# Precedence for PSUM evictions, longer holds in the planner and two zero products at the start

## The chip, the cores and the metric

The kernel runs on one core of one Trainium2 chip. The core has TensorE (PE, matrix products into PSUM), VectorE (DVE), ScalarE (ACT), GpSimd (POOL) and SyncE (SP, which issues DMAs); each takes its own instructions in the order in which the build laid them down. The metric is the device time of one execution in microseconds, the median of the runs shown; lower is better.

## What is computed

Four sequences of 1024 tokens with 256 features pass two layers, in float32. Each of the four sublayers is `x = layernorm(x + f(x))`.

```python
x = ln(x + ssd(x))         # state-space mixing: 2 heads of 128, state 64, causal in a sequence
x = ln(x + gelu(x @ w1 + b1) @ w2 + b2)          # hidden width 1024
x = ln(x + linear_attention(x))  # 16 heads of 16, features exp(clip(norm(q or k) @ omega)), 64 per head
x = ln(x + shared_ffn(x) + routed_ffn(x))  # 2 shared experts, and the best 2 of 8; hidden 512, silu gate
```

The attention is causal: with features `qf`, `kf` each token's output is `sum(qf.kf * v) / sum(qf.kf)` over the tokens up to it, carried from chunk to chunk of 128 tokens as a running state.

## The kernel before

**Tiling.** The 4096 tokens are 8 blocks of 512 (4 tiles of 128). All of a block's activations stay in SBUF (`xs[i]`). The state-space part (`ssd_block`) and the feed-forward (`ffn_block`) work on blocks, the attention on 16 half blocks `hb` (`attn_front`, `attn_back`), `attn_tail` turns the result and computes the router's logits. Then `dispatch` and `invert` sort tokens by expert, the routed part (`slot_tiles`) works through 69 tiles of 128 sorted tokens, and the shared experts' products are cut into small jobs (`shared_jobs`) that are put wherever PE would otherwise be idle: blocks 0 to 2 ("early") and 3 to 5 ("amid") before the routed tiles, 6 and 7 ("late") after them. The jobs form one chain. A block's output products come after the load for the next block, and the amid blocks wait for the last attention projection (`proj_end[15]`), as they use the attention's PSUM banks.

**PSUM.** Until the routed part, PSUM is two pools of banks of 128 x 512 floats: 6 banks in pool 0 (state-space, attention, amid jobs) and 2 in pool 1 (feed-forward, early jobs). A product writes a bank, then ScalarE or VectorE copies or combines it into SBUF (an eviction), and the bank can be written again.

**The order on PE** is laid down by a planner, `trace_tasks`. Each piece of PE work is a `Task` with a cost, a rank, what it comes after (with a waiting time each), a pool and a number of banks, and a hold: the time for which its banks are counted as taken after its end, 1.5 if nothing is said. The planner keeps a clock, takes the task that can start first (the lower rank at equal starts) and so writes PE's instructions in that order:

```python
start = max([d.end + wait for d, wait in task.after], default=0.0)
for k in range(task.banks):
    start = max(start, free[task.pool][k] - task.cost * k / task.banks)
```

**The order on VectorE, ScalarE and GpSimd** is chosen by the tile framework's scheduler until the routed part ends: among instructions that could run, by its own estimate, the one that was written earlier goes first. `tc.high_priority(400)` lets an instruction count as written 400 places earlier.

**Names used below** (lines of the kernel before). In the feed-forward: `ps_txT` (transposes, L206) is copied to `xT` (L208); `ps_h` (L441) goes through Gelu to `hT` (L444); `ps_f` (L453) is added to `x` (L461). In the attention: `ps_txTa` (L206) to `xTa` (L208); `ps_qk` (L502) to `qk` (L505), squared, normalised through `rsqrt` and turned: `ps_qkT` (L550), copied to `qkT` (L551); `ps_p` (L564) to the features `qf`, `kf`, half by VectorE (L574) and ScalarE's exponential (L575), half by ScalarE's Relu (L577), exponential (L578) and VectorE (L579); `ps_sc` (L611) masked to `sc` (L620 to L623); `ps_k` (L633) to `kt` (L634); `ps_o` (L650) to `oraw` (L658); `ps_s` (L672) into `state` (L680, L682); `ps_kv` (L688) to `kv` (L689); `ps_to` (L695) divided into `o` (L698 to L701); `ps_oT` (L708) to `oT` (L710); `ps_w` (L715) added to `x` (L717). In the tail: `ps_txTr` (L206) to `xTr` (L208), `ps_l` (L758). Shared jobs: `ps_g` (L941), silu `sl` (L949), `gT` (L950), `ps_e` (L959), added to `x` (L968). The first products of all are `ps_bc` (L288), from `wx_sb` and the transposed input `xt`. ScalarE loads a table (`ACT_TABLE_LOAD`) when it passes between Gelu, Silu and the exponential; copies and Relu need none. `rsqrt` is a guess by integer arithmetic and three Newton steps, 11 VectorE instructions.

**The end.** The last block's jobs are written in a fixed order on PE, VectorE and ScalarE: after the addition L968 of its third tile come the layernorm sums and scales of the first three tiles, then the addition of the fourth.

Of the kernel before, what the change touches and what calls it, by code (L numbers as in the profile page):

```python
# [27 lines left out]
ALU = mybir.AluOpType  # L28
# [48 lines left out]
def two_layers(ctx: ExitStack, tc: tile.TileContext, x, xT, vecs, cols, wx, w1, w2, wqkv, wout, om, rw, moe, out):  # L77
# [42 lines left out]
    rw_sb = const.tile([P, KC, VW], F32, name="rw_sb")  # L120
    nc.sync.dma_start(out=wx_sb, in_=wx)
    nc.sync.dma_start(out=xts[0], in_=xT[0])
    nc.sync.dma_start(out=vec0, in_=vecs[:NVEC0].partition_broadcast(P))
# [59 lines left out]
    def rsqrt(v, shape, tag):  # L183

        r = sm.tile(shape, F32, tag=f"{tag}_r", name=f"{tag}_r")
        s = sm.tile(shape, F32, tag=f"{tag}_s", name=f"{tag}_s")
        nc.vector.tensor_single_scalar(s.bitcast(I32), v.bitcast(I32), 1, ALU.logical_shift_right)  # L187
        nc.vector.tensor_scalar(r.bitcast(I32), s.bitcast(I32), -1.0, float(0x5F3759DF), ALU.mult, ALU.add)  # L188
        for _ in range(3):
            nc.vector.scalar_tensor_tensor(s, r, -0.5, r, ALU.mult, ALU.mult)  # L190
            nc.vector.tensor_mul(s, s, v)  # L191
            nc.vector.scalar_tensor_tensor(r, s, 1.5, r, ALU.add, ALU.mult)  # L192
        return r

    def transposed(t, i, tiles, n, engines):


        width = len(tiles) * P
        engines = list(engines)
        for c0 in range(0, KC, 512 // width):  # L200
            chunks = range(c0, min(KC, c0 + 512 // width))
            ps = bank(f"ps_t{t.name}_{c0}", n)
            at = 0
            for c in chunks:
                for j in tiles:
                    nc.tensor.transpose(ps[:, at : at + P], xs[i][:, j, c * P : (c + 1) * P], ident)  # L206
                    at += P
            engines.pop(0)(t[:, c0 : chunks[-1] + 1, :].rearrange("p c t -> p (c t)"), ps[:, :at])  # L208
        return t
# [219 lines left out]
    def ffn_block(i, before, wk):  # L429
# [16 lines left out]
        def outputs(j):  # L446
            if j == 0:
                b2 = vec0[:, _VEC["b2"]].unsqueeze(1).to_broadcast([P, NT, D])
                nc.gpsimd.tensor_add(xs[i], xs[i], b2)
            if j % 2 == 0:  # L450
                v.ps = bank(f"ps_f{i}_{j}", 1).rearrange("p (s d) -> p s d", s=2)
            for m in range(HID0 // P):
                nc.tensor.matmul(  # L453
                    v.ps[:, j % 2, :],
                    v.hT[:, m, j * P : (j + 1) * P],
                    w2_sb[:, m, :],
                    start=(m == 0),
                    stop=(m == HID0 // P - 1),
                )
            if j % 2 == 1:  # L460
                nc.vector.tensor_add(xs[i][:, j - 1 : j + 1, :], v.ps, xs[i][:, j - 1 : j + 1, :])  # L461
            if j == NT - 1:
                layernorm(i)

        r = 10.0 + i
        last = Task(turn_x, 0.9, r, [(ssd_end[i], 10.0), (before, 0.0)], 1, 2)
        wait = 4.0
# [19 lines left out]
    def attn_front(hb, wk):  # L487
# [11 lines left out]
        def project(j):  # L499
            ps = bank(f"ps_qk{hb}_{j}", 0)  # L500
            for k in range(KC):
                nc.tensor.matmul(  # L502
                    ps, v.xT[:, k, j * P : (j + 1) * P], wqkv_sb[:, k, : 2 * D], start=(k == 0), stop=(k == KC - 1)
                )
            nc.vector.tensor_add(v.qk[:, j, :], ps, bq[:, : 2 * D])  # L505
            sq = wk.att.tile([P, 2 * D], F32, tag="sq", name=f"sq{hb}_{j}", bufs=2)
# [34 lines left out]
        def turn_qk(s):  # L541

            if s == 1:
                v.qkT = wk.att.tile([P, 4, TH], F32, tag="qkT", name=f"qkT{hb}", bufs=1)
            ps = bank(f"ps_qkT{hb}_{s}", 0)
            for q in range(2):
                for j in range(NJ):
                    at = (q * NJ + j) * P
                    c = 2 * s + q
                    nc.tensor.transpose(ps[:, at : at + P], v.qk[:, j, c * P : (c + 1) * P], ident)  # L550
            nc.scalar.copy(v.qkT[:, 2 * s : 2 * s + 2, :].rearrange("p c t -> p (c t)"), ps)  # L551

        def features(s):
# [17 lines left out]
            for r in range(4):  # L571
                f = ft[:, r].rearrange("p q t -> p (q t)")
                if r % 2 == 0:
                    nc.vector.tensor_scalar(f, ps[r], fcap, ffloor, ALU.min, ALU.max)  # L574
                    nc.scalar.activation(f, f, AF.Exp, bias=fbias[:, s : s + 1])  # L575
                else:
                    nc.scalar.activation(f, ps[r], AF.Relu, bias=fcap, scale=-1.0)  # L577
                    nc.scalar.activation(f, f, AF.Exp, bias=ecap[:, s : s + 1], scale=-1.0)  # L578
                    nc.vector.tensor_scalar_max(f, f, elow[:, s : s + 1])  # L579

        r = 5.0 + 0.1 * hb
        used = used_end.get(hb - 2)
        t_x = Task(turn_x, 0.45, r, [(qk_end.get(hb - 2), 0.0), (ffn_end[i], 10.0), (constants, 0.0), (attention, 0.0)], 0, 1)
        t_q = Task(lambda: project(0), 1.8, r, [(t_x, 3.5)], 0, 1)
        t_q = Task(lambda: project(1), 1.8, r, [(t_q, 0.0)], 0, 1)
        t_v = Task(values, 1.8, r + 0.1, [(t_x, 3.0), (used, 0.0)], 0, 1)
        t_k = Task(lambda: turn_qk(1), 0.45, r + 0.2, [(t_q, 12.0), (feat_end.get(hb - 1), 0.0)], 0, 1)
        t_q = qk_end[hb] = Task(lambda: turn_qk(0), 0.45, r + 0.2, [(t_k, 0.0)], 0, 1)
        t_k = Task(lambda: features(1), 0.95, r + 0.3, [(t_k, 5.0), (used, 0.0)], 0, 4, 4.5)
        feat_end[hb] = Task(lambda: features(0), 0.95, r + 0.3, [(t_q, 5.0), (t_k, 0.0), (t_v, 0.0)], 0, 4, 4.5)  # L590

    def attn_back(hb, wk):
# [5 lines left out]
        def scores(j):  # L598
# [7 lines left out]
            for q in range(2):  # L606
# [9 lines left out]
                for s in range(2):  # L616
                    t_s = t[:, 4 * s : 4 * s + 4, :]
                    ps_s = ps[s].rearrange("p (r t) -> p r t", t=P)
                    if (q, s) == (0, 0):
                        nc.scalar.copy(t_s, ps_s)  # L620
                        nc.gpsimd.tensor_mul(t_s, t_s, mask)  # L621
                    else:
                        nc.vector.tensor_mul(t_s, ps_s, mask)  # L623
                sc[j].append(t)

        def turn_keys(j):
# [3 lines left out]
            for q in range(2):  # L630
                ps = bank(f"ps_k{hb}_{j}_{q}", 0)
                for r in range(4):
                    nc.tensor.transpose(ps[:, r * P : (r + 1) * P], kf[:, r, q, tok], ident)  # L633
                nc.scalar.copy(kt[j][:, q, :], ps)  # L634

        def outputs(j):
# [20 lines left out]
            for n in range(2):  # L657
                nc.scalar.copy(  # L658
                    o[j].rearrange("p (g n t) -> p n g t", n=2, t=P)[:, n],
                    ps_o[n][:, : 2 * P].rearrange("p (g t) -> p g t", t=P),  # L660
                )

        def advance(j):
# [17 lines left out]
            else:  # L681
                nc.vector.tensor_add(state, ps_v[:, : 4 * NF], state)  # L682

        def turn_state(j):

            ps_kv = bank(f"ps_kv{hb}_{j}", 0)
            for q in range(2):
                nc.tensor.transpose(ps_kv[:, q * P : (q + 1) * P], state[:, q * 2 * NF : (q + 1) * 2 * NF], ident)  # L688
            nc.scalar.copy(kv.rearrange("p f e -> p (f e)"), ps_kv[:, : 2 * P])  # L689

# [14 lines left out]
        def turn_back(j):  # L705
# [3 lines left out]
            oT[j] = wk.att.tile([P, KC, P], F32, tag="oT", name=f"oT{hb}_{j}", bufs=2)  # L709
            nc.scalar.copy(oT[j].rearrange("p c t -> p (c t)"), ps[:, :D])  # L710

        def project(j):
# [3 lines left out]
            x_j = xs[i][:, j0 + j, :]  # L716
            nc.vector.tensor_add(x_j, ps[:, :D], x_j)  # L717
            if hb % 2 == 1 and j == NJ - 1:
                layernorm(i)

        for j in range(NJ):
# [5 lines left out]
            t_c = Task(lambda j=j: scores(j), 1.8, r, [(feat_end[hb], 7.0), (before.get("o"), 0.0)], 0, 4, 2.5)  # L727
            t_k = Task(lambda j=j: turn_keys(j), 0.9, r + 0.01, [(feat_end[hb], 6.0), (before.get("s"), 0.0)], 0, 2, 2.0)
            t_o = Task(
# [6 lines left out]
            t_t = at_tile[n]["to"] = Task(lambda j=j: turn(j), 0.45, r + 0.04, [(t_o, 1.5), (far.get("oT"), 0.0)], 0, 1, 2.5)  # L736
            t_t = at_tile[n]["oT"] = Task(lambda j=j: turn_back(j), 0.25, r, [(t_t, 2.0), (far.get("w"), 0.0)], 0, 1)
            t_w = at_tile[n]["w"] = Task(lambda j=j: project(j), 0.9, r, [(t_t, 2.5)], 0, 1)
        used_end[hb], proj_end[hb] = t_o, t_w

    def attn_tail(i, wk):
# [26 lines left out]
        r = 5.3 + 0.2 * i  # L768
        t_x = turn_end[i] = Task(turn_x, 0.9, r, [(proj_end[2 * i + 1], 10.0), (tail_end.get(i - 1), 0.0)], 0, 2)
        t_x = Task(logits, 0.5, r, [(t_x, 5.0)], 0, 1)  # L770
# [299 lines left out]

    def last_norm(i, tiles):

# [4 lines left out]
        r = None  # L1077

        def sums():
            st = sm.tile([P, NT, 6], F32, tag="ln_st", name=f"ln_st{i}_{tiles[0]}")  # L1080
            for k, j in enumerate(tiles):
                nc.vector.bn_stats(st[:, k, :], xs[i][:, j, :])  # L1082
                nc.vector.bn_aggr(mv[:, k, :], st[:, k, :])  # L1083

# [6 lines left out]
        def finish():  # L1091
# [7 lines left out]
            )  # L1099

        return sums, scales, finish

# [41 lines left out]
    early, amid, late = [0, 1, 2], [3, 4, 5], [6, 7]  # L1144
    with tc.manual_schedule(engines={mybir.EngineType.PE}):
        for i in range(NBLK):
            ssd_block(i, wk0)
# [97 lines left out]
    with tc.manual_schedule(  # L1245
# [8 lines left out]
        for _, kind, *_, piece in jobs:  # L1254
# [9 lines left out]
            if n in norm:  # L1264
                parts.extend(last_norm(*norm[n]))
                if len(parts) == 3:
                    parts.pop(0)()
            if n == 22:
                ends = last_norm(NBLK - 1, whole[:-1])
                ends[0]()  # L1270
                ends[1]()
# [74 lines left out]
```

## Time and profile before

| | us |
|---|---|
| median of 3 runs | 1566.04 |
| lowest, highest | 1563.34, 1570.9 |
| the profiled execution, its own time | 1570.37 |
| its span, first to last instruction | 1568.6 |
| PE busy in the span | 1493.9 |
| VectorE, ScalarE, GpSimd busy | 761.8, 599.2, 420.3 |
| mean granted TensorE clock (1 is full) | 0.983 |

The profile is of one execution. "Waits" name who waited for whom, with the total in us, the number of times and the longest one. In a timeline, the bracket behind an instruction is the idle time of its engine just before it and what ended that. One float32 matrix product shows as two passes (`x2`), a transpose as one. The granted clock of a stage is the mean over it.

### The profile page before, as it was taken

How to read it: one execution, taken by the hardware profiler on the slowest of the kernel's cores; microseconds unless marked ns; L12 is line 12 of the kernel's file. 1: busy time of each engine (PE TensorE's matmuls, PEld its weight loads, DVE VectorE, ACT ScalarE, POOL GpSimd, SP SyncE). 2: the span in 40 equal slices, each digit the busy share in tenths (PEclk: the TensorE clock that was granted, in tenths of full speed). 3: DMA queues.
4: the chain of work that ended last, by engine and by line, in shares of the span. 5: the costliest groups of instructions: out<-in, count | busy, mean ns of one | idle time of the engine just before them, and what ended most of it. 6: DMA issues, size and time to landing. Idle time of an engine off the chain costs nothing. (4 is left out here: it accounts for less than half of the span.)

```text
span 1568.6 us, 25398 instructions
## 1 busy us (share of the span) xinstructions
PE 1493.9 (95%) x9700; PEld 970.0 (62%) x9700; DVE 761.8 (49%) x2411; ACT 599.2 (38%) x1056; POOL 420.3 (27%) x456
## 2 busy tenths in 40 slices
PE   8999989999999989989999999999999999999997
PEld 5566647575857665755765765556666666666554
DVE  5977735665656475575455456122222222222264
ACT  3463373436364625446547411111222222222132
POOL 5623302322122121221110004012444444443100
PEclk9999999999999999999999999999999999999999
DMA  9000000000000000030101043041223223232431
GB/s 328 1 1 1 1 1 2 27 2 1 28 1 15 15 1 28 2 122 1 48 8 55 15 166 136 24 151 41 46 47 46 46 45 47 45 47 35 91 104 54
DMA packets 49654, 73.55 MB, mean 47 GB/s; under 512 B 8416, under 2 KB 42208, under 8 KB 48000
## 3 DMA queue, kind: packets, MB, share of 16 engines
q1 hardware_dynamic: 35856, 52.19, 9.4%
q0 software_dynamic: 13248, 18.17, 7.5%
q8 instruction: 80, 1.31, 0.4%
q10 hardware_dynamic: 432, 1.57, 0.3%
q14 instruction: 38, 0.31, 0.1%
HBM read 45.93 MB, written 25.99 MB: 46 GB/s over the span
## 5 line engine op out<-in xcount | busy, mean ns | idle before, releaser
L1013 PE MATMUL ps_ge<-w,xeT 128*128 x552 | 248.5, 593 | 1.0 <-issue 1.0
L941 PE MATMUL ps_g<-xTs,w 128*128 128x512 f32 x512 | 225.9, 594 | 5.4 <-ACT sl L949 2.6
L941 PEld LDWEIGHTS ps_g<-xTs,w 128*128 128x128 f32 x512 | 95.6, 190 | 119.3 <-issue 106.1
L1013 PEld LDWEIGHTS ps_ge<-w,xeT 128*128 128x128 f32 x552 | 99.5, 190 | 100.6 <-issue 100.6
L1044 POOL DMA_INDIRECT acc<-ye,back x69 | 109.4, 1585 | 110.1 <-DVE xew L1000 75.6
L1023 DVE TENSOR_TENSOR ge<-se,ps_ge 128x512 f32<-128x512 f32 x69 | 47.5, 688 | 178.7 <-PE ps_ge L1013 175.8
L441 PE MATMUL ps_h<-xT,w_sb 128*128 128x512 f32 x256 | 123.5, 627 | 9.1 <-ACT hT L444 5.4
L1035 PE MATMUL ps_ye<-w2e,geT 128*128 x552 | 130.7, 380 | 0.9 <-DVE geT L1030 0.9
L988 POOL DMA_INDIRECT xe<-xt,sent x69 | 68.2, 989 | 228.7 <-PE ps_xe L996 166.3
L453 PE MATMUL ps_f<-w_sb,hT 128*128 128x256 f32 x512 | 117.5, 384 | 0.0
L959 PE MATMUL ps_e<-w,gT 128*128 128x256 f32 x512 | 114.6, 380 | 2.1 <-DVE x L968 2.1
L621 POOL TENSOR_TENSOR sc<-sc,mask_le 128x512 f32<-128x512 f32 x32 | 40.9, 1278 | 275.3 <-ACT sc L620 275.3
L959 PEld LDWEIGHTS ps_e<-w,gT 128*128 128x128 f32 x512 | 96.1, 190 | 18.9 <-DVE x L968 3.7
L1035 PEld LDWEIGHTS ps_ye<-w2e,geT 128*128 128x128 f32 x552 | 99.6, 190 | 12.2 <-ACT ye L1043 1.1
L453 PEld LDWEIGHTS ps_f<-w_sb,hT 128*128 128x128 f32 x512 | 96.8, 192 | 15.9 <-issue 3.4
L950 DVE TENSOR_TENSOR gT<-sl,ps_g 128x512 f32<-128x512 f32 x64 | 43.9, 686 | 115.0 <-PE ps_g L941 92.4
L949 ACT ACTIVATE sl<-ps_g 128x512 f32<-128x512 f32 x64 | 38.0, 596 | 156.7 <-PE ps_g L941 143.4
L441 PEld LDWEIGHTS ps_h<-xT,w_sb 128*128 128x128 f32 x256 | 49.7, 201 | 65.5 <-issue 54.8
L1021 ACT ACTIVATE se<-ps_ge 128x512 f32<-128x512 f32 x69 | 41.3, 599 | 121.5 <-PE ps_ge L1013 121.5
L623 DVE TENSOR_TENSOR sc<-ps_sc,mask_le 128x512 f32<-128x512 f32 x96 | 62.7, 685 | 37.5 <-PE ps_sc L611 30.4
L611 PE MATMUL ps_sc<-qf,kf 64*128 64x128 f32 x1024 | 68.0, 281 | 0.6 <-ACT kf L577 0.5
L1000 DVE TENSOR_TENSOR xew<-xe,nth 128x1 f32<-128x1 f32 x69 | 11.0, 160 | 118.2 <-ACT ye L1043 109.9
(257 smaller groups left out, 2485.5 us busy)
## 6 DMA issues: line engine op xcount, KB each, us to landing
w<-in_moe SPq DMA_DIRECT2D x8, 1024.0 KB, 9.1
xt<-in_xT SPq DMA_DIRECT2D x8, 512.0 KB, 9.6
x<-in_x SPq DMA_DIRECT2D x8, 512.0 KB, 10.8
xt<-x SPq DMA_DIRECT2D x8, 512.0 KB, 3.7
td<-xTr SPq DMA_DIRECT2D x16, 256.0 KB, 2.5
w2e<-in_moe SPq DMA_DIRECT2D x8, 512.0 KB, 7.6
x<-acc SPq DMA_DIRECT2D x8, 512.0 KB, 8.4
out<-x SPq DMA_DIRECT2D x7, 512.0 KB, 2.9
```

Source lines behind the costliest of these rows:

```text
L441: nc.tensor.matmul(ps, w1_sb[:, k, m * P : (m + 1) * P], v.xT[:, k, :], start=(k == 0), stop=(k == KC - 1))
L453: nc.tensor.matmul(v.ps[:, j % 2, :], v.hT[:, m, j * P : (j + 1) * P], w2_sb[:, m, :], start=(m == 0), stop=(m == HID0 // P - 1),)
L611: nc.tensor.matmul(ps[s][:, r * P : (r + 1) * P], kf[rows, r, q, tok], qf[rows, r, q, tok], start=True, stop=True)
L623: nc.vector.tensor_mul(t_s, ps_s, mask)
L941: nc.tensor.matmul(ps[s], w[e][:, 2 * s + k, m * P : (m + 1) * P], xT[i][:, k, :], start=(k == 0), stop=(k == KC - 1),)
L950: nc.vector.tensor_mul(gT[i, e][:, m, :], sl, ps[1])
L959: nc.tensor.matmul(ps, gT[i, e][:, m, j * P : (j + 1) * P], w2e[:, m, :], start=(e == 0 and m == 0), stop=(e == NSH - 1 and m == HID // P ...
L988: nc.gpsimd.indirect_dma_start(out=xe, out_offset=None, in_=xt, in_offset=bass.IndirectOffsetOnAxis(ap=sent[:, s : s + 1], axis=0),)
L1013: nc.tensor.matmul(pg[a], xeT[s][:, k, :], w13[:, bass.ds(e * (4 * HID) + (2 * a + k) * HID, HID)], start=(k == 0), stop=(k == KC - 1),)
L1023: nc.vector.tensor_mul(ge[s], se, pg[1])
L1035: nc.tensor.matmul(ps[:, :D], geT[s][:, m, :], w2[:, bass.ds(of[s] * (2 * HID) + m * D, D)], start=(m == 0), stop=(m == HID // P - 1),)
L1044: nc.gpsimd.indirect_dma_start(out=acc, out_offset=bass.IndirectOffsetOnAxis(ap=back[:, s : s + 1], axis=0), in_=ye, in_offset=None, compu ...
```

## The change

- Evictions in feed-forward and attention are written under `soon()`, which is `tc.high_priority(400)`: the copies of all transposed `x`, the additions L461, L505, L682, L717, the copies L551, L634, L658, L689, L710, the first reading of `ps_p` (L574, L577) and of `ps_sc` (L620, L623). The Gelu of `hT` (L444), the division into `o` (L698 to L701), the values (L535) and the state-space evictions are not.
- Holds in the planner go from 1.5 to 2.5 up to 4.5 for tasks that turn or project; 2.0 to 3.0 for `turn_keys`.
- Before everything else PE multiplies a tile of zeros by itself twice, into a bank that nothing reads.
- The first loads (`wx_sb`, `xt` of block 0) are split in halves, one of them issued on ScalarE's queue.
- `rsqrt` takes a cubic step and a Newton step: 9 instructions.
- The layernorm sums of the last block's first three tiles are written each after its own tile's addition.

```diff
-    nc.sync.dma_start(out=wx_sb, in_=wx)
-    nc.sync.dma_start(out=xts[0], in_=xT[0])
+    for n in range(2):
+        (nc.scalar, nc.sync)[n].dma_start(out=wx_sb[:, :, n, :], in_=wx[:, :, n, :])
+        nc.sync.dma_start(out=xts[0][:, n, :], in_=xT[0][:, n, :])
...
-        for _ in range(3):
-            nc.vector.scalar_tensor_tensor(s, r, -0.5, r, ALU.mult, ALU.mult)
-            nc.vector.tensor_mul(s, s, v)
-            nc.vector.scalar_tensor_tensor(r, s, 1.5, r, ALU.add, ALU.mult)
+        nc.vector.tensor_mul(s, r, r)
+        nc.vector.tensor_mul(s, s, v)
+        nc.vector.scalar_tensor_tensor(s, s, -10.0 / 3.0, s, ALU.add, ALU.mult)
+        nc.vector.scalar_tensor_tensor(r, s, 5.0, r, ALU.add, ALU.mult)
+        nc.vector.scalar_tensor_tensor(s, r, -0.5 * 0.375**3, r, ALU.mult, ALU.mult)
+        nc.vector.tensor_mul(s, s, v)
+        nc.vector.scalar_tensor_tensor(r, s, 1.5 * 0.375, r, ALU.add, ALU.mult)
...
+    def soon():
+
+        return tc.high_priority(400)
...
-            engines.pop(0)(t[:, c0 : chunks[-1] + 1, :].rearrange("p c t -> p (c t)"), ps[:, :at])
+            with soon():
+                engines.pop(0)(t[:, c0 : chunks[-1] + 1, :].rearrange("p c t -> p (c t)"), ps[:, :at])
...
-        last = Task(turn_x, 0.9, r, [(ssd_end[i], 10.0), (before, 0.0)], 1, 2)
+        last = Task(turn_x, 0.9, r, [(ssd_end[i], 10.0), (before, 0.0)], 1, 2, 4.0)
...
-            nc.scalar.copy(v.qkT[:, 2 * s : 2 * s + 2, :].rearrange("p c t -> p (c t)"), ps)
+            with soon():
+                nc.scalar.copy(v.qkT[:, 2 * s : 2 * s + 2, :].rearrange("p c t -> p (c t)"), ps)
...
-                    nc.scalar.activation(f, ps[r], AF.Relu, bias=fcap, scale=-1.0)
+                    with soon():
+                        nc.scalar.activation(f, ps[r], AF.Relu, bias=fcap, scale=-1.0)
...
-        t_q = Task(lambda: project(0), 1.8, r, [(t_x, 3.5)], 0, 1)
-        t_q = Task(lambda: project(1), 1.8, r, [(t_q, 0.0)], 0, 1)
+        t_q = Task(lambda: project(0), 1.8, r, [(t_x, 3.5)], 0, 1, 2.5)
+        t_q = Task(lambda: project(1), 1.8, r, [(t_q, 0.0)], 0, 1, 2.5)
...
-        t_k = Task(lambda: turn_qk(1), 0.45, r + 0.2, [(t_q, 12.0), (feat_end.get(hb - 1), 0.0)], 0, 1)
-        t_q = qk_end[hb] = Task(lambda: turn_qk(0), 0.45, r + 0.2, [(t_k, 0.0)], 0, 1)
+        t_k = Task(lambda: turn_qk(1), 0.45, r + 0.2, [(t_q, 12.0), (feat_end.get(hb - 1), 0.0)], 0, 1, 4.5)
+        t_q = qk_end[hb] = Task(lambda: turn_qk(0), 0.45, r + 0.2, [(t_k, 0.0)], 0, 1, 4.5)
...
+        idle = wkf.tile([P, TB], F32, name="idle")
+        nc.vector.memset(idle, 0.0)
+        ps = bank("ps_idle", 0)
+        for _ in range(2):
+            nc.tensor.matmul(ps, idle[:, :P], idle, start=True, stop=True)
...
-            if n == 22:
-                ends = last_norm(NBLK - 1, whole[:-1])
-                ends[0]()
-                ends[1]()
+            if n == 20:
+                ends = last_norm(NBLK - 1, whole[:-1], True)
+            if 20 <= n < 23:
+                ends[0](n - 20, n - 20)
+            if n == 22:
+                ends[1]()
```

The other edits are of the same kinds: `soon()` around the evictions listed, and longer holds of the attention's `turn_x` (3.5), `turn_keys` (3.0), `turn_back` (2.5) and the tail's `turn_x` (4.5).

## The prediction

> **What bounds the kernel now.** I read the page's table of busy time first, then the stages, then what TensorE waited for, then one wait in the timeline.
>
> ```profile
> PE 1493.9 (95%) x9700; PEld 970.0 (62%) x9700; DVE 761.8 (49%) x2411; ACT 599.2 (38%) x1056; POOL 420.3 (27%) x456
> ```
>
> TensorE (PE) is the bound; 75 us of the span are not its. The stages show where (PE, PEld, DVE, ACT, POOL busy, then granted clock):
>
> ```profile
> 60.00:190.00 130.00, 125.52 (x618) 84.76 (x617) 98.50 (x424) 62.24 (x102) 50.45 (x84) 0.98 0.00 1
> 190.00:900.00 710.00, 661.13 (x6448) 454.75 (x6447) 401.56 (x1155) 365.48 (x612) 140.06 (x138) 0.97 0.06 21
> 900.00:1070.00 170.00, 168.60 (x610) 100.92 (x608) 62.06 (x144) 23.37 (x39) 24.45 (x19) 1.00 0.30 112
> 1070.00:1475.00 405.00, 402.31 (x1516) 248.50 (x1516) 108.17 (x269) 99.52 (x206) 169.15 (x130) 1.00 0.28 44
> ```
>
> From 900 to 1475 us PE is full at full clock: nothing is to be had there. Attention and feed-forward, 190 to 900 us, hold 49 us of gaps, and their clock is 0.97. A lost 0.03 of 710 us is 21 us; with 0.02 of 130 and 0.01 of 48 (12 to 60 us, 0.99) the low clock costs about 24 us before 900 us. It follows the gaps. PE's waits between 12 and 900 us sum to 55.6 us; the largest:
>
> ```profile
> PE ps_k L633 <- ACT qkT L551: 8.2, 4, 2.5
> PE ps_p L564 <- ACT qkT L551: 7.1, 6, 2.9
> PE ps_h L441 <- ACT hT L444: 5.4, 4, 2.1
> PE ps_oT L708 <- DVE o L701: 4.0, 2, 3.6
> PE ps_h L441 <- DVE ln_s L191: 3.5, 1, 3.5
> PE ps_p L564 <- DVE x L717: 3.2, 3, 1.8
> PE ps_l L758 <- ACT xTr L208: 3.0, 4, 0.7
> PE ps_w L715 <- ACT oT L710: 2.9, 1, 2.9
> ```
>
> Most are waits for a PSUM bank to be emptied or for the copy out of it. One of the first kind:
>
> ```profile
> 445.22 1.28 ACT L444 ACT_TABLE_LOAD   x1
> 446.51 1.27 ACT L444 ACTIVATE hT<-ps_h,col 128x512 f32<-128x512 f32 x2
> 447.67 0.59 ACT L551 COPY qkT<-ps_qkT 128x512 f32<-128x512 f32 x1
> 448.31 0.90 PE L633 MATMUL ps_k<-ident,kf 128*128 128x128 f32 x3 [2.53 <-ACT qkT L551]
> ```
>
> The copy itself is 0.59 us; a table load and two Gelus stood ahead of it, and PE, which wanted that bank for `ps_k`, lost 2.53 us.
>
> **The change part by part**, against the profiled execution (1570.37 us, span 1568.6).
>
> *Precedence and holds.* Some 630 evictions get precedence on ScalarE and VectorE; longer holds make the planner put other products between two uses of a bank. In the order of the new build, at the wait just shown, both `qkT` copies stand next to each other with no Gelu ahead, and `ps_k` of that half block comes 6.0 us of PE work after the `ps_qkT` whose bank it takes, where it was 1.3. I added up PE work (start to start: 0.43 us per pass of 512 columns, 0.22 of 256, 0.11 of 128, from the page) between the last write of a bank of pool 0 and its next use: reuses with under 2 us between fall from 30 to 16, under 1.5 us from 17 to 4; in pool 1, under 2 us from 11 to 5. Table loads on ScalarE fall from 82 to 76, 6 x 1.28 = 7.7 us of its time.
>
> Of the 55.6 us, 39.1 wait on something that now has precedence or on the work queued with it (`qkT` 15.3; L717 3.2; `xTr`, `xTa` 4.4; `oT` 2.9; L574 and L577 7.2; L461 1.9; 4.2 put down to a layernorm, 3.5 of which is the `xT` copy behind it: it is 17 places earlier in the VectorE order). By the counts, what is left lies between 4/17 and 16/30; I take a third: 26 saved, bounds 18 and 30. 13.1 us wait on things without precedence (`hT` Gelu 5.4, `o` 4.0, shared products 3.7); fewer tight reuses in pool 1 and fewer table loads help, evictions put ahead hurt: 3 saved, bounds -4 and 7. 3.4 us belong to the state-space blocks: nothing.
>
> *What the new order adds.* The shared products that fill PE are used up earlier: 48 of their banks are written before the last `ps_w` where it was 40, and the next ones wait for that `ps_w`. So the last half block runs bare: `ps_oT` directly after `ps_to`, twice (0.16 + 0.24 + 0.42 us of L698 to L701 and the handovers, 1.3 each), `ps_w` after `ps_oT` (0.37 + handovers, 0.7), `ps_to` and `ps_o` with 0.7 to 1.5 us between (1.1 together): 4.4 us lost, bounds 0 and 8. Dispatch also comes later: `ps_id` stands 22 us of PE work further back, `ps_xe0` only 2. They were 50 us apart (1015.2 and 1065.7); 28 us still cover the expert loads that follow `ps_id` on SP (12.8 us to landing at most, 4 us to issue), so nothing; below about 17 us it would cost one for one.
>
> *Clock.* The low periods follow long gaps, and these sit in the 39.1. I take 60% of 24 us: 14.6, bounds 4 (only the worst periods go) and 20.
>
> *Start.* Halved loads and two zero products:
>
> ```profile
> 5.11 6.54 PE L288 MATMUL ps_bc<-xt,wx_sb 128*128 128x512 f32 x8 [5.11 <-DMA xt<-in_xT]
> 11.92 1.88 PE L288 MATMUL ps_bc<-xt,wx_sb 128*128 128x512 f32 x4
> ```
>
> The first eight passes took 0.82 us each, later ones 0.47: 2.8 us too long. PE starts at 5.11; with the zeros it starts as soon as VectorE has cleared their operand, about 1.4, and four slow passes end at 4.7. If the clock rises with the time that PE has been busy (5.8 us here), it does so about 3.6 us earlier, worth half, 1.8; the halves bring the first tokens 0.4 earlier, as the zeros allow no more. VectorE, busy 42 of the 48 us that follow, is fed by this chain and moves with it: 2.2, bounds 0 and 3.2. The half load issued on ScalarE stands before its first table load; its first use is at 7.73, so nothing. [...]
>
> *Shorter rsqrt, split sums.* Two of 11 steps go, 49 times: 98 x 0.16 to 0.23 us of VectorE, beside PE everywhere but at the end; there 2 x 0.20 = 0.4. The sums of two tiles (4 x 0.3) move out of the chain ahead of the last addition, L968 at 1561.40; but PE itself ends at 1561.08, so 0.3. If PE did not bind, it would be 1.2. Together 0.7.
>
> *DMAs moved.* On SP, writes of `acc` and one `xTs` load swap places with the stores of later blocks; the load still stands 32 us of PE work ahead of its first product. Nothing.
>
> Sum: 26 + 3 - 4.4 + 14.6 + 2.2 + 0.7 = 42 us. The profiled execution is 4.3 above the median of 1566.04, inside the runs' own spread; so I take 42 off the median: 1524 us.
>
> **A rule against it.** VectorE and ScalarE take instructions in order here: the `qkT` copy above could not pass the Gelus. [...] An eviction put ahead of ready work therefore holds everything behind it until its product is done. By that rule alone, precedence moves waits rather than removing them, and the sum would keep only the holds' share, say half.
>
> **The rivals.**
> Slower: the Gelu of `hT` and the exponentials lost their places. Four pairs of `ps_h` in each of eight blocks need their bank back; now 4 of them waited, 5.4 us in all. If each of the 32 waited for two evictions and a table load, 2 x 0.6 + 1.28 = 2.5 us, less the 0.9 that the other bank's two products last, that is 51 us, against 42 saved: 1575. It decides from 1.3 us per pair on. For it: VectorE is 57% and ScalarE 51% busy in the stage, with many loads of the table. Against it: the new order has fewer table loads, and Gelus come in unbroken pairs.
> Waits come back elsewhere: PE is fed by a chain of dependences, and an early eviction only shows the next late thing. Then half of gaps and clock return: 42 - 20 = 22, 1545. For it: `o` (L701) and `hT` have no precedence.
> Only start and end count, the order in the middle being no better: 3 us, 1563. Against it: the counts of tight reuses.
> Nearly all gaps close and the clock stays up: 30 + 7 + 20 + 3.2 + 0.7 with no bare tail: 61, 1505.
>
> **How the numbers follow.** About 1524 (1508 to 1542) 0.60; waits elsewhere, up to 1558, 0.17; only the ends 0.06; slower 0.09; nearly all 0.08. The range of 1505 to 1556 leaves out the slower case, the ends-only case and part of the last. Half a per cent (8 us) is about what a measurement can tell here: faster 0.85, same 0.06, slower 0.09.
>
> **What would show it.** Right: the `ps_k` and `ps_p` waits on `qkT` (15.3 us) under 4, PE's waits before 900 us near 30, the clock of that stage at 0.99, passes of 0.43 us from about 7 us on, a bare stretch of some 4 us before the last `ps_w`, the last `L968` at PE's end. Wrong: new waits of `ps_h` on `hT`, of `ps_sc` or `ps_o` on features, or a gap ahead of `ps_xe0`.

## The result, and the profile after

The changed kernel takes 1592.12 us (median of 4 runs, 1590.69 to 1593.84) against 1567.07 in the 4 runs of before: a ratio of 1.016, 95% interval 1.0131 to 1.0189. It is 25 us slower; 42 us faster was forecast. The profiled execution took 1593.48, its span is 1591.6, 23.0 more than before.

Line numbers are now those of the changed kernel, 10 to 25 higher: `ps_h` L451 to `hT` L454, `ps_qkT` L562 to `qkT` L564, `ps_p` L577, `ps_k` L650, `o` L722, `ps_oT` L729, `ps_w` L737, `ps_g` L964, `sl` L972, `ps_e` L982, `x` L991. First the page's table of busy time, then the stages (PE, PEld, DVE, ACT, POOL busy, granted clock, DMA share, GB/s):

```profile
PE 1501.8 (94%) x9704; PEld 970.1 (61%) x9704; DVE 753.3 (47%) x2314; ACT 590.3 (37%) x1050; POOL 419.4 (26%) x456
```

```profile
60.00:190.00 130.00, 127.37 (x650) 86.68 (x649) 98.32 (x417) 62.78 (x103) 52.65 (x87) 1.00 0.00 1
190.00:900.00 710.00, 648.44 (x6040) 437.99 (x6037) 380.75 (x1041) 335.44 (x572) 136.57 (x134) 0.97 0.06 21
900.00:1070.00 170.00, 161.92 (x902) 98.89 (x901) 72.30 (x177) 41.96 (x68) 24.25 (x20) 0.98 0.26 92
1070.00:1475.00 405.00, 403.38 (x1518) 250.23 (x1517) 107.34 (x271) 96.14 (x199) 164.51 (x128) 1.00 0.29 51
```

VectorE, ScalarE and GpSimd are busy for less time than before. PE has the four passes over the zeros more (3.8 us) and is busy 7.9 us longer, part of which is time at half clock (58.0 us, before 47.8). From 190 to 900 us PE has 62 us of gaps where it had 49, at the same clock of 0.97, and the attention now ends 36 us later: the last `ps_w` at 947.7, before at 911.3. What PE waited for between 12 and 1060 us, the largest and the one that the change aimed at:

```profile
PE ps_h L451 <- ACT hT L454: 21.5, 11, 3.6
PE ps_g L964 <- ACT sl L972: 15.5, 7, 3.7
PE ps_oT L729 <- DVE o L722: 7.4, 5, 3.5
PE ps_e L982 <- ACT sl L972: 4.8, 2, 3.1
PE ps_w L737 <- ACT oT L732: 3.9, 3, 2.9
...
PE ps_p L577 <- ACT qkT L564: 1.1, 1, 1.1
```

The waits on `qkT` fell from 15.3 to 1.1 us, as forecast. Those on Gelu and Silu, ScalarE's two evictions in the feed-forward and the shared jobs, which have no precedence, rose from 8.0 to 43.2 (all lines on `hT` and `sl`). Everything together: 56.5 before, 75.2 now. The timeline shows how, on ScalarE and PE:

```profile
595.25 0.73 ACT L593 ACTIVATE qf<-qf,ecap 128x512 f32<-128x512 f32 x1
...
595.87 0.72 ACT L589 ACTIVATE qf<-qf,fbias 128x512 f32<-128x512 f32 x1
...
596.49 0.71 ACT L593 ACTIVATE qf<-qf,ecap 128x512 f32<-128x512 f32 x1
597.10 0.57 ACT L564 COPY qkT<-ps_qkT 128x512 f32<-128x512 f32 x1
597.56 0.60 ACT L218 COPY xTa<-ps_txTa 128x512 f32<-128x512 f32 x1
...
598.16 1.28 ACT L454 ACT_TABLE_LOAD   x1
599.46 1.26 ACT L454 ACTIVATE hT<-ps_h,col 128x512 f32<-128x512 f32 x2
...
600.20 1.22 PE L451 MATMUL ps_h<-xT,w_sb 128*128 128x512 f32 x1 [3.38 <-ACT hT L454]
```

ScalarE has no gap here. The `ps_h` products ended at 594.9. Three exponentials and two copies with precedence stand ahead of their Gelu, which then needs its own table load, and the first Gelu is done near 600.1, 5.2 us after its product. PE had 2.0 us of other products and then waited 3.38 us for the bank. It is the stall that the prediction shows, with the places of `qkT` and `hT` exchanged.

**How the time adds up.** The trace's clock records show half clock in periods of 3.41 us each or multiples of it: 14 of them before (47.8 us), 17 after (58.0), each counted as a loss of half its length. So the waits give +18.7 and the clock +5.1: 23.8, where the span grew by 23.0. The same sum meets the spans of the runs below within 3.3 us, but for e14 and e15, whose spans are 6.0 and 5.4 us shorter than it says.

### The profile page after: what moved, and what is told of

It reads as the page before. It is cut to its first block, busy times and chain, and to the rows that moved or that the text cites. A ratio compares the mean times of both kernels' runs of the same rounds, so it can differ in the third digit from the quotient of the medians.

```text
span 1591.6 us, 25296 instructions
## 1 busy us (share of the span) xinstructions
PE 1501.8 (94%) x9704; PEld 970.1 (61%) x9704; DVE 753.3 (47%) x2314; ACT 590.3 (37%) x1050; POOL 419.4 (26%) x456
## 5 line engine op out<-in xcount | busy, mean ns | idle before, releaser
L964 PE MATMUL ps_g<-xTs,w 128*128 128x512 f32 x512 | 228.4, 599 | 16.3 <-ACT sl L972 15.5
L964 PEld LDWEIGHTS ps_g<-xTs,w 128*128 128x128 f32 x512 | 95.7, 191 | 128.7 <-issue 104.4
L451 PE MATMUL ps_h<-xT,w_sb 128*128 128x512 f32 x256 | 127.7, 645 | 21.5 <-ACT hT L454 21.5
L982 PE MATMUL ps_e<-w,gT 128*128 128x256 f32 x512 | 118.0, 388 | 7.5 <-ACT sl L972 4.8
L982 PEld LDWEIGHTS ps_e<-w,gT 128*128 128x128 f32 x512 | 98.6, 194 | 26.6 <-ACT sl L972 5.3
L451 PEld LDWEIGHTS ps_h<-xT,w_sb 128*128 128x128 f32 x256 | 50.8, 207 | 79.1 <-issue 50.3
L972 ACT ACTIVATE sl<-ps_g 128x512 f32<-128x512 f32 x64 | 38.1, 597 | 148.6 <-PE ps_g L964 138.3
L1066 ACT ACTIVATE ye<-ps_ye,xew 128x256 f32<-128x256 f32 x69 | 32.6, 473 | 92.6 <-PE ps_ye L1058 92.6
```

What stands on the lines that cost most here:

```text
L451: nc.tensor.matmul(ps, w1_sb[:, k, m * P : (m + 1) * P], v.xT[:, k, :], start=(k == 0), stop=(k == KC - 1))
L964: nc.tensor.matmul(ps[s], w[e][:, 2 * s + k, m * P : (m + 1) * P], xT[i][:, k, :], start=(k == 0), stop=(k == KC - 1),)
L982: nc.tensor.matmul(ps, gT[i, e][:, m, j * P : (j + 1) * P], w2e[:, m, :], start=(e == 0 and m == 0), stop=(e == NSH - 1 and m == HID // P ...
```

## The experiments

Times are medians; ratios are against the kernel before on the same chip (1567.1 for the first row, 1568.3 to 1568.6 for the others). "Waits" are PE's between 12 and 1060 us, "half" the time at half clock after the first rise, both in us. These two come from one profiled execution each, which lies within 3.2 us of the median, but for e6 (1577.5, so 5.5 below).

| kernel | us | ratio [95%] | waits | half |
|---|---|---|---|---|
| whole change | 1592.1 | 1.016 [1.013, 1.019] | 75.2 | 58.0 |
| e3: without precedence | 1592.7 | 1.016 [1.014, 1.017] | 72.6 | 54.6 |
| e2: without the longer holds | 1561.8 | 0.996 [0.995, 0.998] | 54.0 | 37.5 |
| e4: start, rsqrt and end alone | 1575.1 | 1.003 [1.001, 1.004] | 59.3 | 54.6 |
| e7: e4 with the rsqrt of before | 1569.7 | 1.000 [0.998, 1.002] | 59.5 | 44.4 |
| e9: before, with precedence alone | 1566.6 | 1.000 [0.998, 1.001] | 55.7 | 44.4 |
| e16: e2 with the rsqrt of before | 1566.2 | 0.999 [0.998, 1.000] | 56.3 | 44.4 |
| e5: e2 with the holds of the attention's front | 1568.7 | 1.000 [0.999, 1.002] | 56.8 | 37.5 |
| e6: e2 with the holds of keys, back, tail | 1583.0 | 1.009 [1.006, 1.012] | 64.8 | 51.2 |
| e11: e2 with the hold of the keys | 1570.2 | 1.001 [0.999, 1.002] | 59.0 | 41.0 |
| e12: e2 with the hold of the tail | 1567.3 | 1.000 [0.998, 1.001] | 59.6 | 37.5 |
| e8: whole change, pool 1 held for 4.5 too | 1574.3 | 1.004 [1.002, 1.005] | 58.2 | 54.6 |
| e1: whole change, precedence for Gelu and Silu too | 1582.5 | 1.009 [1.007, 1.010] | 67.7 | 51.2 |
| e10: e2, precedence for Gelu and Silu too | 1562.9 | 0.998 [0.996, 0.999] | 57.1 | 37.5 |
| e13: whole change, Relu for Gelu and Silu | 1542.3 | 0.984 [0.982, 0.986] | 41.6 | 23.9 |
| e14: e2, Relu for Gelu and Silu | 1534.2 | 0.979 [0.976, 0.981] | 36.5 | 27.3 |
| e15: e4, Relu for Gelu and Silu | 1539.6 | 0.981 [0.979, 0.984] | 42.8 | 23.9 |

**Holds or precedence: e1 to e4.** Four kernels tell holds and precedence apart. e1 gives the two evictions that were left out their precedence:

```diff
+                with soon():
                     nc.scalar.activation(v.hT[:, m, :], ps, AF.Gelu, bias=col[:, m : m + 1])
...
+            with soon():
                 nc.scalar.activation(sl, ps[0], AF.Silu)
                 nc.vector.tensor_mul(gT[i, e][:, m, :], sl, ps[1])
```

> The changed kernel, with precedence also for the Gelu of hT, the Silu and the product gT. TensorE's order is the same as in the changed kernel; ScalarE's order has 92 table loads where it had 76. Theory P (precedence pushed Gelu and Silu back in ScalarE's queue, because they alone had none): the waits of ps_h on hT and of ps_g and ps_e on sl (43 us in the changed kernel) fall below 15 us, time 1555 to 1570. Theory H (the longer holds put the ps_h and ps_g products next to the features, where ScalarE has exponentials to do in any order): these waits stay above 30 us, time 1585 to 1600.

e2 puts all holds back (1.5, `turn_keys` 2.0) and leaves the rest of the change:

```diff
-        t_k = Task(lambda: turn_qk(1), 0.45, r + 0.2, [...], 0, 1, 4.5)
+        t_k = Task(lambda: turn_qk(1), 0.45, r + 0.2, [...], 0, 1)
```

> The changed kernel with the holds of before: TensorE's order is that of before, but for the two zero products. Precedence, start, rsqrt and end stay. Theory P: waits of ps_h on hT and ps_g on sl over 30 us, time 1580 or more. Theory H: these waits stay near the 8 us of before and the waits on qkT fall from 15 us to under 8, time 1540 to 1555.

e3 makes precedence empty and leaves the holds; e4 does both:

```diff
     def soon():
-        return tc.high_priority(400)
+        return ExitStack()
```

> The changed kernel without precedence: the longer holds, start, rsqrt and end stay. Theory P: waits on hT and sl near the 8 us of before, time 1550 to 1567. Theory H: waits on hT and sl 35 us or more, time 1590 or more.

> Only the start, the shorter rsqrt and the split sums of the end; holds and precedence of before. Both theories: the forecast's 2.9 us less than before, so 1562 to 1566, waits on hT and sl as before (8 us).

Measured, with start, rsqrt and end in all four: neither 1575.1, precedence alone 1561.8, holds alone 1592.7, both 1592.1. The holds cost 17.6 us without precedence and 30.3 with it; precedence gains 13.3 under the old holds and nothing under the new. So the loss is that of the holds, with or without precedence. Neither theory was met in full: e3 has the time of theory H, but its waits on `hT` and `sl` are 24.8 us and not 35; e1 (17.8 us of them) and e2 (22.5) lie between the two in waits and time; e4 is 9 us above its forecast. The waits of e3, the first four, and of e2 on Gelu, Silu and `qkT`:

```profile
PE ps_h L451 <- ACT hT L454: 12.7, 11, 2.0
PE ps_p L577 <- ACT qkT L564: 9.3, 5, 2.9
PE ps_g L964 <- ACT sl L972: 8.3, 7, 1.8
PE ps_oT L729 <- DVE o L722: 7.1, 4, 3.5
```

```profile
PE ps_h L451 <- ACT hT L454: 11.6, 7, 2.8
PE ps_g L964 <- ACT sl L972: 8.4, 5, 3.7
...
PE ps_k L650 <- ACT qkT L564: 1.7, 4, 1.1
...
PE ps_p L577 <- ACT qkT L564: 0.2, 1, 0.2
```

In PE's new order Gelu, Silu, `qkT` and `o` all come late; with precedence the waits on `qkT` fall by 8.2 us, and those on `hT` and `sl` rise by 18.4. e1 confirms the exchange from the other side: `hT` and `sl` fall by 25.4 us, waits on the features `qf` rise by 12.6, and the gain is 9.6.

**Precedence alone, and with Gelu: e9 and e10.** e9 is the kernel before with `soon()` around the same evictions, e10 is e2 with the edit of e1. PE's order is that of before in both.

> Precedence alone on the kernel before: holds, start, rsqrt and end are those of before, and so is TensorE's order. With the other edits in, precedence was worth 13 us (1575.1 without it, 1561.8 with it). If that holds alone: 1553 to 1558. If it only undid what the shorter rsqrt had done to the orders of VectorE and ScalarE: 1562 to 1567.

> The changed kernel with the holds of before, and precedence also for Gelu, Silu and gT; 86 table loads on ScalarE where that without it has 76. With the longer holds this was worth 10 us. If the waits on hT and sl (22 us with old holds) simply go: 1548 to 1556. If the 10 table loads more (12.8 us of ScalarE) and the features behind them cost as much: 1558 to 1570, with new waits of ps_sc on the features.

e9's waits, the first two:

```profile
PE ps_h L447 <- ACT hT L450: 10.0, 6, 2.6
PE ps_g L960 <- ACT sl L968: 8.4, 5, 3.7
```

Waits on `qkT` fell by 13.4 us, those on `hT` and `sl` rose by 12.8; total 56.5 and 55.7, and the time is that of before. In e10 `hT` and `sl` fall by 18.6, `qkT` and `qf` rise by 18.5; 1562.9 against 1561.8. Both times are those of the second forecast made for them, though e10's new waits are on `qkT` too. In the timeline of the section on the result ScalarE let nothing pass: the Gelus whose products ended at 594.9 stood behind five other instructions until 598.2. In these two pairs precedence chose who waits and not how long.

**Start, end and rsqrt: e7 and e16.** e7 is e4, and e16 is e2, each with the three Newton steps of before:

```diff
-        nc.vector.tensor_mul(s, r, r)
...
+        for _ in range(3):
+            nc.vector.scalar_tensor_tensor(s, r, -0.5, r, ALU.mult, ALU.mult)
...
```

> Of the change only the start (zero products, halved loads) and the split sums; rsqrt has its three Newton steps, holds and precedence are those of before. If the shorter rsqrt cost time by changing VectorE's and ScalarE's order in the attention (9.8 us were lost there with the three end edits, after a start that was 2.9 us ahead at the first ps_txTr): 1563 to 1567, and still 2 us or more ahead at the last ps_w. If the start or the zero products do it: 1572 or more.

> Precedence, start and end with the holds and the rsqrt of before. Without precedence the shorter rsqrt lost 5.4 us in the middle (1569.7 to 1575.1) though PE's order was the same, as VectorE's and ScalarE's order came out differently. If that loss belongs to the operations themselves, this kernel is 5 us faster than the 1561.8 with the new rsqrt: 1557. If it is only an accident of the order that the scheduler then chose, it is not: 1560 to 1567.

e7 is the start and the split sums alone: 1.000 [0.998, 1.002], worth nothing that can be measured; 1569.7 lies between its two forecasts. Between e7 and e4 the shorter rsqrt loses 5.4 us, though it is two instructions fewer; between e16 and e2 it gains 4.4. PE's order is the same in all four; what differs is the order in which the scheduler then laid down VectorE's and some of ScalarE's work. By the same table precedence is worth 3.5 us with the old rsqrt (e7 to e16, not clear of the noise) and 13.3 with the new. About 5 us either way is what the scheduler's order decided by itself in these two pairs (the second case of e16's forecast), so the 13 us of precedence are a favourable draw as well as an effect.

**Which holds: e5, e6, e11, e12, e8.** Each adds part of the new holds to e2, as in

```diff
-            t_k = Task(lambda j=j: turn_keys(j), 0.9, r + 0.01, [...], 0, 2, 2.0)
+            t_k = Task(lambda j=j: turn_keys(j), 0.9, r + 0.01, [...], 0, 2, 3.0)
```

e5 has those of the attention's `turn_x`, `project` and `turn_qk`; e6 those of `turn_keys`, `turn_back` and the tail's `turn_x`; e11 only `turn_keys`, e12 only the tail's.

> Precedence, start, rsqrt and end as in the changed kernel; of the longer holds only those of the attention's front (turn_x 3.5, project 2.5, turn_qk 4.5). TensorE's order differs from that with old holds; 40 shared banks are written before the last ps_w, as before, and ScalarE has 66 table loads. Theory F (the loss comes with filler being used early, the shared products running out before the last half block): no loss, 1555 to 1565. Theory G (pool 0 counted as taken for longer while Gelu's and Silu's banks of pool 1 are not, so filler is put into the time in which ScalarE does the features): the waits on hT and sl rise above 30 us, time 1578 or more.

> As the one with the front's holds, but only those of turn_keys (3.0), turn_back (2.5) and the tail's turn_x (4.5) are longer. 48 shared banks are written before the last ps_w, as in the changed kernel. Theory F: most of the loss is here, 1580 or more, and a bare stretch before the last ps_w of 4 us or more. Theory G: little loss, 1562 to 1572, as turn_qk's holds, which stand beside the features, are those of before.

> The changed kernel with old holds, but turn_keys holding its two banks for 3.0 and not 2.0. 44 shared banks before the last ps_w. If the loss follows the number of shared banks used early (40 at 1561.8, 48 at 1583.0): about 1570 to 1575. If turn_keys is the hold that matters: 1578 or more; if the tail's: 1560 to 1566.

> The changed kernel with old holds, but the tail's turn_x holding its two banks for 4.5 and not 1.5. 46 shared banks before the last ps_w. If the loss follows that number: about 1575 to 1580. If the tail's hold is the one that matters: 1578 or more; if that of turn_keys: 1560 to 1566.

Against e2: front +6.9, keys +8.5, tail +5.5, keys with back and tail +21.2; front and e6 together 28.1 of the 30.3. Each of the three tested groups makes the kernel slower, so no single one is the culprit. The hold of `turn_back` and the feed-forward's own, 4.0, were not run alone. e6 is as theory F says, and e5 lies between the two theories. The number of shared banks used early is not what decides: with 46 of them e12 should have cost more than e11 with 44, and it did not.

e8 leaves the whole change and lengthens what the planner holds in pool 1, where Gelu and the early shared jobs empty the banks:

```diff
-            last = Task(lambda n=n: hidden(range(2 * n, 2 * n + 2)), 3.5, r + 0.1 * n, [(last, wait)], 1, 2, 2.2)
+            last = Task(lambda n=n: hidden(range(2 * n, 2 * n + 2)), 3.5, r + 0.1 * n, [(last, wait)], 1, 2, 4.5)
...
-            jobs.append(Task(job, cost, 100.0, after, n, banks, 2.0))
+            jobs.append(Task(job, cost, 100.0, after, n, banks, 4.5))
```

> The changed kernel with longer holds for pool 1 too: 4.5 for ps_h (was 2.2) and for the shared jobs (was 2.0), as long as those given to turn_qk. Theory G: the planner then leaves Gelu and Silu their time, waits on hT and sl fall from 43 us below 15, time 1550 to 1570. Theory F: the filler is used in other places, but as early (46 banks before the last ps_w): 1580 or more.

It takes back 17.8 of the 25 us: `hT` 22.9 to 0.7 (0.2 of it `ps_h`, in one place), `sl` 20.3 to 6.8:

```profile
PE ps_g L964 <- ACT sl L972: 6.8, 4, 2.6
...
PE ps_f L463 <- ACT hT L454: 0.5, 1, 0.5
...
PE ps_h L451 <- ACT hT L454: 0.2, 1, 0.2
```

These waits are as theory G says, the time is not. The reading that fits: the planner's new order had brought the two `ps_h` products back to pool 1 while their Gelu stood in the longer queue, as holding pool 0 longer and pool 1 as before took time from the one and gave it to the other. Still, at 1574.3 it is 0.4% slower than the kernel before: other waits (`oT` 7.6, `o` 5.7) and the low clock stay.

**ScalarE's service time, or PE's order: e13, e14, e15.**

```diff
-                nc.scalar.activation(v.hT[:, m, :], ps, AF.Gelu, bias=col[:, m : m + 1])
+                nc.scalar.activation(v.hT[:, m, :], ps, AF.Relu, bias=col[:, m : m + 1])
...
-            nc.scalar.activation(sl, ps[0], AF.Silu)
+            nc.scalar.activation(sl, ps[0], AF.Relu)
```

> The whole change, with Relu in place of the Gelu of hT and of the Silu of the shared jobs; these two functions are left out of the computation, the shapes and PE's order are those of the whole change (1592). Relu needs no table, so the 1.28 us loads fall from 76 to 6 in the whole program. Theory A, the longer holds lose their 30 us through ScalarE's service time (Gelu and Silu stand behind table loads, copies and exponentials): the 43 us of waits on hT and sl fall under 10, the whole run comes to 1560 or less, and within 10 us of its fellow with the old holds. Theory B, PE's new order itself is worse (its dependences lie closer together, filler is used up early, the last half block is bare): it gains 15 us or less and stays 20 us or more above its fellow with the old holds; the waits come back on other names (oT, o, features).

> Precedence, start and end of the change with the holds of before (1562), with the same two functions replaced by Relu. PE's order is that of the kernel before. Theory A: its 22.5 us of waits on hT and sl go too, but it had fewer to lose: 1545 to 1552, and the gap to the run with the longer holds shrinks from 30 to under 10 us. Theory B: the same 1545 to 1555, and the gap stays at 20 us or more.

> Start, rsqrt and end alone (1575), with the same two functions replaced by Relu: no precedence, holds of before. With the tables gone this says what precedence is worth when ScalarE is quick. If precedence gains only because the copies of qkT no longer stand behind a table load and two Gelus, the 13 us between this kernel and the one with precedence shrink to under 4. If it gains by order alone, they stay at 8 or more.

These three kernels leave Gelu and Silu out of the computation. Relu takes the same time here as Gelu (0.69 us a time in both traces) but needs no table: 6 loads are left of 76, and with those of Gelu and Silu the exponential's between them go too. The page of e13 and its waits on the two:

```profile
PE 1483.9 (96%) x9704; PEld 963.0 (63%) x9704; DVE 747.5 (49%) x2314; ACT 497.7 (32%) x980; POOL 419.6 (27%) x456
```

```profile
PE ps_h L451 <- ACT hT L454: 3.7, 4, 1.3
PE ps_g L964 <- ACT sl L972: 2.5, 3, 1.1
```

ScalarE is busy for 92.6 us less, of which the 70 loads, at 1.28 us each in the trace of the whole change, are 90; taking them away brings 49.8 us, from an engine that was 37% busy. The gap between the longer and the old holds shrinks from 30.3 to 8.1 us, and that between with and without precedence from 13.3 to 5.4, which the intervals don't tell from nothing and which lies between the two cases of e15's forecast. That is theory A, up to a rest: some 22 of the 30 us that the new order lost came with ScalarE's table loads, behind which Gelu and Silu, and others behind them, had to wait. These sizes are rough. PE's order is the same in each pair, but the scheduler placed some 2% of ScalarE's and 3% of VectorE's instructions otherwise, and such a shift was worth 5 us above; e14 is also 11 us faster than the least that was expected. Some 8 us are left, perhaps for PE's order itself: between the seventh group of `ps_txTr` and the last `ps_w`, where filler is short, e13 still has 3.5 us of gaps and e14 none.

**The better kernel** is e2: precedence, start, rsqrt and end with the old holds, 1561.8 us, 0.996 of before; e10, at 1562.9, can't be told from it.

## Why the prediction was wrong

**What bounds.** Right: PE, waits on evictions between 190 and 900 us, and the clock behind them.

**Precedence and holds, 26 us saved (bounds 18 and 30).** The size was nearly right: without `hT`, `sl` and `o` (12.0 before, 50.6 after) and the state-space blocks (3.4 and 4.1), the waits fell from 41.1 (of which the forecast had 39.1) to 20.5: 20.6 saved. The reason was half wrong, so the size is in part luck. The counts of tight reuses gave the holds the credit; the same rest is 23.8 us in e2, with precedence and the old holds, and 37.3 in e3, with the holds alone, so precedence did most of it.

**Waits without precedence, 3 saved (bounds -4 and 7).** This is the step that failed. `hT` and `sl` went up by 35.2 and `o` by 3.4: 38.6 lost, 42 us away from the forecast. The bound was taken from the few waits that there were, and not from the evictions that could come to wait. Two things feed it. Precedence hands the time over: with PE's order unchanged the total moved by 0.8 us (e9). And the longer holds, booked as a gain because reuses under 2 us fell (30 to 16 in pool 0, 11 to 5 in pool 1), cost 17.6 to 30.3 us. Those counts were of PE's work alone. A reuse 2 or 3 us away is still late when the Gelu comes 5.2 us after its product, as in the timeline above.

**"Fewer table loads".** True (82 to 76) and used twice, for the gain and against the slower rival. The number of loads says little: e10 has 86 and is among the fastest. By the timelines, what counts is whether a load stands ahead of something that PE wants, as the 1.28 us ahead of the Gelu at 599.5, for which PE waited 3.38.

**The bare last half block, -4.4.** Right in mechanism and within its bounds: between the seventh `ps_txTr` group and the last `ps_w` PE's gaps went from 0.8 to 7.4 us, 6.6 more (they are part of the waits counted above). `ps_oT` directly after `ps_to`, forecast at 1.3 a time:

```profile
938.89 0.41 PE L729 MATMUL ps_oT<-ident,o 128*128 128x128 f32 x2 [1.71 <-DVE o L722]
...
945.59 0.41 PE L729 MATMUL ps_oT<-ident,o 128*128 128x128 f32 x2 [1.30 <-DVE o L722]
946.46 1.25 PE L737 MATMUL ps_w<-wout_sb,oT 128*128 128x256 f32 x4 [0.46 <-ACT oT L732]
```

**Dispatch, nothing.** Right: `ps_id` came 44.4 us later and `ps_xe0` 23.7, so 29.8 us of cover were left (28 forecast), with no gap of PE between the two.

**Clock, +14.6 (4 to 20).** Wrong sign: -5.1. That it follows the gaps was right: in the traces of before and after, each low period up to PE's last product begins within 5 us of the start of a gap of PE of 0.8 to 3.7 us. The gaps went the other way. The clock records of both traces have a granted share of 1 or of 0.5, and every low period between the first rise and PE's last product is 3.41 us long or a multiple of it.

**Start, +2.2.** PE's first instructions:

```profile
1.53 3.78 PE L1180 MATMUL ps_idle<-idle 128*128 128x512 f32 x4 [1.53 <-DVE run L870]
5.11 1.10 PE L298 MATMUL ps_bc<-xt,wx_sb 128*128 128x512 f32 x2
6.39 2.84 PE L298 MATMUL ps_bc<-xt,wx_sb 128*128 128x512 f32 x6 [0.18 <-DMA xt<-in_xT]
```

As forecast, the zeros start at 1.5 and passes take 0.47 from 6.39 on. The clock rises at 5.3 (10.9 before), after 3.7 us of work and not the 5.8 that the forecast took. The first `ps_y` comes 1.5 us earlier. But e7, which has the start and the split sums, ends where the kernel before does: the gain was used up in the state-space stage. The first `ps_txT` behind it comes at 62.6 to 66.8 us in the kernels with this start (64.7 in the whole change, 66.8 in e7) and at 65.7 before it.

**rsqrt and the end, +0.7.** From the last `ps_e` to the end it is 6.7 us where it was 7.5, so 0.8, and the last addition follows PE's end directly. Beside PE "nothing" was wrong: the shorter rsqrt changed the order on VectorE, and with it came -5.4 or +4.4.

**The rule against it** was the better forecast: an eviction put ahead holds what stands behind it (the Gelu at 599.5 was done 5.2 us after its product). "Precedence moves waits rather than removing them" is what e9 and e10 show. The half that was to be kept for the holds was wrong.

**The sum.** 20.6 - 38.6 - 0.7 (state-space) - 5.1 (clock) + 0 (start) + 0.8 (end) = -23.0; the span grew by 23.0.

**The rivals.** "Slower" named the mechanism (Gelu loses its place) and the sign, and got 0.09. It priced 32 pairs at 1.6 us, 51 us; measured were 11 waits of `ps_h` of 2.0 each, and as much again on Silu, which it left out. It also kept the 42 saved, where 20.6 us of waits were and the clock got worse. Its argument against, that Gelus come in unbroken pairs with fewer loads, is what the timeline above refutes: the pair is unbroken, and late. "Only start and end" forecast 1563; e4 gave 1575.1 and e7 1569.7.

**Left open.** Which detail of VectorE's order costs or gains the 5 us of the rsqrt, how the last 8 us of the holds' loss divide between the bare last half block and the rest, and whether an order that groups ScalarE's work by table under the real functions would keep part of e14's gain: none of these was tried.

## What to carry to other kernels

When a wait names an eviction, read what the evicting engine did in the 5 us before it: if it was busy without a gap, giving that eviction precedence may only name another wait, as in e9 and e10, and a sum of saved waits has to book what the displaced ones cost. An engine that is 37% busy in the mean can still be the server that sets the bound in its busy stretches, and its fixed costs there (here the table load, 1.28 us where a copy of 128x512 takes 0.57 to 0.60) can be worth more than places in its queue (49.8 us in e13, nothing in e9). Ask of a planner that spaces bank reuses whether its holds stand for the eviction's real time in the queue, for every pool, and test each edit with the others on and off: orders that a scheduler chooses moved this kernel by 5 us in either direction from an edit that made one helper two instructions shorter.

## What was not expected of the hardware

- A large part of the time of the table loads came back as kernel time: 70 loads of 1.28 us gone (90 us), 49.8 us faster (e13), 27.5 with the old holds (e14), on an engine that had 1001 us free. At 598.16 the load is 1.28 us long, directly after a copy and 0.02 us ahead of the Gelu.
- How early the clock rises with two zero products varies, with the same first instructions: from 4.5 us (e1, e15) to 7.6 us (e12), so 3.0 to 6.1 us after PE's first product. Without them it was at 10.9 (before) and 11.4 (e9).
- No low period between the first rise and PE's last product was shorter than 3.41 us in these runs. So a gap that one of them follows costs some 1.7 us beside itself, an estimate from half of 3.41, as in the sum above: 14 such lengths before, 17 after, 7 in e13.
